# A hybrid of selective scan, attention and spectral filters: softplus in pairs, mixed matrices requested sooner, sums of y beside a filter's projection

## The chip, the cores and the metric

The kernel runs on one core of one Trainium2 chip. Its engines work in parallel, each through its own queue in order: TensorE (PE; its weight loads are listed as PEld), VectorE (DVE), ScalarE (ACT), GpSimd (POOL), and SyncE (SP), which here issues nearly all DMAs. The metric is the device time of one execution in microseconds (us). A change of under 0.2% can hardly be told from none.

## The reference, cut to what matters

Four images of 48 x 48 positions with 128 channels pass through a selective scan in four directions, self-attention, and a spectral filter layer. All numbers are float32.

```python
# layer 0, per image (L = 2304 positions, d = 256, K = 4 directions, N = 16 states, R = 8)
xz = einsum('bhwc,ec->bhwe', gn(x), in_proj_w);  xin, z = split(xz)
xc = silu(depthwise_conv3x3(xin))
xs = stack([rows, columns, rows reversed, columns reversed of xc])
x_dbl = einsum('bkdl,kcd->bkcl', xs, x_proj_w);  dts_r, Bs, Cs = split(x_dbl)
dt = softplus(einsum('bkrl,kdr->bkdl', dts_r, dt_proj_w) + dt_proj_b)
def step(h, inp):                         # for each position
    h = h * exp(dt_l * A) + (dt_l * u_l) * B_l
    y = einsum('bkdn,bkn->bkd', h, C_l)
...
x = x + out_proj(layernorm(sum over directions of y + Ds * xs) * silu(z))
# layer 1
t = t + softmax(ln(t) @ ln(t).T) @ ln(t)
# for each of four prefixes of the sequence, 16 filters phi, both signs:
U_plus, U_minus = causal convolutions of u = ln(t) with phi (and with alternating sign)
out = einsum('btkd,k,kde->bte', U_plus, s, Mpp) + einsum('btkd,k,kde->bte', U_minus, s, Mpm)
out = out + three shifted products of u with M_u
t = t + the prefixes' outs, weighted
```

## The kernel before

**Stages.** The program goes through the images (batches b = 0 to 3) one after the other. Each has a *scan stage* (`scans`) and then a stage of the scan's epilogue and attention, in which the prologue of the next image is worked in. Spectral filters of image b - 1 (`stu`) are done on PE beside the scans of image b, for b = 1 to 3; beside the scans of image 0 PE makes the mixed matrices `G` of all filters (`mixture`) and writes them to memory (`gd`). The filters of image 3 come alone at the end (`stu3`). Instructions stand in the order in which the Python code issues them; each engine works through its own part of that order.

**Scans.** An image has 24 *chunks* (4 directions x 6 stretches of 384 positions), and a chunk 8 *units* (2 halves of the channels x 4 groups of states), so 192 units in a stage. A unit is four scans on DVE (L517) over decays `exp(dt * A)` that ACT makes (L510), one instruction for each scan. The decays lie in the *ring*: 5 banks of PSUM for image 0, 4 for the others. The same banks take the spread rows of B (L493, a copy on ACT) and the small products of the chunk preparation. The scan's input dt*x*B is made by DVE (L501) or, for three of eight units, by POOL (same line). After the scans POOL multiplies by C (L527), and PE sums over the states (`sum_c`, L535, four matmuls with 32 columns each side by side); after four units DVE adds the sum to `ya` (L547; for image 0, ACT copies, L545). Scan tiles `s` are six deep, so a late sum keeps a tile from its next unit.

**Preparation.** `Chunk.prep` is a generator that runs 15 steps, each of three calls, over the units before its chunk; `LEAD` says that it starts 17 units ahead. It projects x to `xd` (L411, L418; for directions 2 and 3 `xd` is read back, L400), makes dt in two halves (L428, copy L431 into `re`), applies softplus (L440), multiplies by x (L458, DVE, into the other half of `re`), stores both as `dtdud` (L447), and loads them spread over the partitions as `rep` (L452, 8 DMAs per chunk). The rows B and C are requested by `fetch` (L479), four DMAs for each of 8 tiles `bc0` to `bc7` (one buffer each), as soon as a tile is free. Softplus and exp lie in different tables of ACT: an `ACT_TABLE_LOAD` stands ahead of each softplus and ahead of the next exponential.

**Filters beside the scans.** `stu` has 80 *items* (5 blocks of positions x 16 filters). Item n does: first Toeplitz product `conv(n, 0)` into bank `cx`; the projections of item n - 2 with `G` (`project`, L1224, two matmuls, one for each sign, the second after a call of `fetch` for the next Toeplitz tables `tt`, L1120); second product `conv(n, 2)`, accumulating in the same bank `cx`; third product `conv(n, 1)` in bank `cy`. ACT copies results away (`taken`): after the first product `cx` to `cy` (L1177), which the second product must wait for, after the second (L1184, L1185) and after the third (L1181) into `U`. These copies are issued 500 columns (`LATER`) of PE's later work after their product. `fetch_G` (L1131) requests `G` for item n - 1 after the first product of item n; `G` has two buffers.

**The weave.** In each unit step s, `scans` issues scan 0, work, the product with C of unit s - 1, scan 1, the addition to `ya`, work, scan 2, work, scan 3, the requests of `bc` (`refill`), the sum of unit s - 2 on PE, and work. "Work" is `more(share)`: it pulls pieces of `stu` until the columns done have reached that share of the stage. `prepare(s)` is called three times in the step.

**Before a scan stage.** The first chunks are prepared in the last slots of the attention before: `begin_scans` is called from slot `slots - BEGIN` (BEGIN = 23) on and yields once per slot. A slot is two matmul steps on PE and one exponential on ACT.

Of the kernel before, what the change touches and what calls it, by code (L numbers as in the profile page):

```python
# [15 lines left out]
P = 128  # L16
# [25 lines left out]
COPIES = 3  # L42
SHIFT = 55.0
LATER = 500


class Stage:
# [13 lines left out]
def hybrid_kernel(ctx: ExitStack, tc: tile.TileContext, a: dict, out: bass.AP):  # L61
# [9 lines left out]
    bank = {"turn": 0}  # L71

    ident = wp.tile([P, P], F32, name="ident")
    make_identity(nc, ident)
# [292 lines left out]
    class Chunk:  # L367


        def __init__(self, b, k, c):  # L370
            self.b, self.k, self.lo = b, k, c * CS
            self.name = f"{b}_{k}_{c}"
            self.bc, self.rep = {}, []
            self.rev = k >= 2
            self.first = c == (NCH - 1 if self.rev else 0)
            self.last = c == (0 if self.rev else NCH - 1)

            self.slot = CS if self.rev else 0
            self.at = slice(0, CS) if self.rev else slice(1, CS + 1)

        def prep(self, pool):
# [38 lines left out]
                mm_done(hold)  # L420
            yield from rest()

            re = pool.one.tile([P, NH, 2, CS], F32, tag="re", name=f"re{name}")
            for h in range(NH):
                hold = mm_hold()
                yield
                ps = mm_tile(f"dt{name}_{h}", hold)
                nc.tensor.matmul(ps[:, :CS], dtw[:, k, h * P:(h + 1) * P], xd, start=True, stop=True)  # L428
                yield CS
                yield  # L430
                nc.scalar.copy(re[:, h, 0], ps[:, :CS])  # L431
# [8 lines left out]
            nc.scalar.activation(re[:, :, 0], re[:, :, 0], AF.Softplus)  # L440
            yield
            yield
            yield 0
            d = dram.tile([NH, G4, DL, 2, CS], F32, tag="dtdu", name=f"dtdud{name}")

            def store(h):
                nc.sync.dma_start(d[h].rearrange("g j i t -> (g j) i t"), re[:, h])  # L447

            def load(h):
                rep = pool.rep.tile([P, G4, 2, CS], F32, tag="rep", name=f"rep{name}_{h}")  # L450
# [3 lines left out]

            for h in range(NH):
                x = in_order(xc[h], k, self.lo, CS)
                dt, dx = [re[:, h, i].rearrange("p (r w) -> p r w", w=x.shape[2]) for i in range(2)]
                nc.vector.tensor_tensor(dx, dt, x, ALU.mult)  # L458
            yield
            yield  # L460
            store(0)
# [88 lines left out]
    POOLED = ((0, 3), (1, 1), (1, 3))  # L550
    order = [(k, c) for k in range(K) for c in (range(NCH) if k < 2 else reversed(range(NCH)))]
    quads = [(h, q) for h in range(NH) for q in range(Q4)]
    STEPS = 15
    LEAD = 17
    FETCHED = range(2 * Q4)

    CHUNK_COLS = len(quads) * CS + 3 * CS

    def begin_scans(b, pool):

        chunks = [Chunk(b, k, c) for k, c in order]
        preps = [ch.prep(pool) for ch in chunks]
        for i in range(7):
            next(preps[0])
        for i in range(3 * STEPS - 7):
            if next(preps[0]) is not None:
                yield
        for i in FETCHED:
            chunks[0].fetch(i, pool)
        for i in range(3 * (LEAD - len(quads))):  # L570
            if next(preps[1]) is not None:
                yield
        for i in range(3 * (LEAD - 2 * len(quads))):
            next(preps[2])
        yield chunks, preps

    def scans(b, chunks, preps, front, sp, back, ring, finish, work, work_cols):
# [60 lines left out]
        for s in range(len(units) + 2):  # L638
            real = s < len(units)
            enter(s)  # L640
            prepare(s)
            if real:
                scan(s, 0)
            more((s + 0.25) / len(units))
            next(finish, None)
            if 1 <= s <= len(units):
                units[s - 1].times_c(s == len(units))
            if real:
                scan(s, 1)
# [417 lines left out]
    def stu(b, env, seeds):  # L1067
# [119 lines left out]
        def begin(n):  # L1187
            (lo, hi, place, extra), k = items[n]
            m = 2 if extra else 1

            now["x"] = pool.one.tile([P, 6, P], F32, tag="ux", name=f"ux{b}_{n}")
            nc.sync.dma_start(now["x"][:, 2:, :hi - lo], ud[:, :, 1 + lo:1 + hi])
            nc.sync.dma_start(now["x"][:, :2, :hi - lo], ud[:, 2:, lo:hi])
            now["mu"] = pool.one.tile([P, 2, 3, C], F32, tag="mue", name=f"mue{b}_{n}")
            nc.sync.dma_start(now["mu"][:, :m], mud[:, place:place + m])
            now["T", n] = pool.two.tile([P, 4, C], F32, tag="res", name=f"res{b}_{n}")
# [19 lines left out]
        def project(n):  # L1216
# [3 lines left out]
            for q in range(2):  # L1220
# [54 lines left out]
        fetch_G(n)  # L1275
        for i in (n - 1, n):
            yield from project(i)
            do_late()
# [231 lines left out]

    SB = bass.MemoryType.SB

    BEGIN = 23

    def run(tasks, lag, other):

# [33 lines left out]
    run(prologue(0, turn.one, mm_tile), 3, weights(once.one))  # L1550
    turn.close()
    once.close()
    front = Stage(tc, "f0", "left", one=(1, SB), xd=(3, SB), rep=(3, SB))
    first = begun(begin_scans(0, front))
    begin0.close()
    start_y(0)
    for b in range(B):
# [56 lines left out]
                parts.pop(0)()  # L1614
        if more:
            turn.close()
            front = Stage(tc, f"f{b + 1}", "left", one=(1, SB), xd=(3, SB), rep=(3, SB))
            start_y(b + 1)
            pieces = begin_scans(b + 1, front)
        first = None  # L1620
# [81 lines left out]
```

## Time and profile before

| what | value |
|---|---|
| three executions | 5554.54, 5556.91, 5560.95 us (median 5556.91) |
| profiled execution | 5558.94 us, span 5557.2 us |
| mean granted TensorE clock | 0.932 |
| before the first scan | 0 to 120 us |
| scan stages of images 0 to 3 | 948.5, 985.4, 988.3, 988.5 us |
| between them (epilogue, attention) | 247.1, 241.5, 242.4 us |
| after the last scan (attention, filters of image 3) | 795.5 us |
| DMA issues of SP in the page: bc, rep, dtdud | 3072 of 48 KB, 768 and 192 of 384 KB |
| table loads ahead of softplus and of exponentials | 95 and 89, 1283 ns each |

A profile row names line, engine, instruction, output<-inputs, shape and count. "Idle before" is the time for which the engine stood before such instructions, followed by what ended it. In a table of waits, "PE cx L1161 <- ACT cy L1177" reads: PE stood before matmuls of line 1161 until ACT had done its copy of line 1177. A PE product of float32 shows as two matmul records. The granted clock is near 1.0 in the scan stages of images 1 to 3 and 0.76 in that of image 0.

### The profile page before, as it was taken

What the parts mean: (1) busy time and instruction counts of PE and PEld (TensorE: products, weight loads), DVE (VectorE), ACT (ScalarE), POOL (GpSimd) and SP (SyncE); (2) the same over time, 40 slices, a digit from 0 to 9 for tenths busy, and PEclk for the clock granted to TensorE, in tenths of its full rate; (3) what the DMA queues carried; (4) which work ended last, traced back from release to release, by engine and by line L of the source; (5) the groups of instructions that cost most, each with busy time, mean ns of one, the idle gap of its engine ahead of it and who ended that gap; (6) DMA issues with size and microseconds to landing.
All of it is one profiled execution on the core that took longest, in us unless ns stands there. A gap on an engine that the chain in (4) does not pass through costs nothing. (4 is left out here: it accounts for less than half of the span.)

```text
span 5557.2 us, 73634 instructions
## 1 busy us (share of the span) xinstructions
PE 4768.0 (86%) x23372; PEld 3061.7 (55%) x23372; DVE 4338.2 (78%) x5307; ACT 3327.3 (60%) x6923; POOL 3660.4 (66%) x1882
## 2 busy tenths in 40 slices
PE   3566555698899999897899999997999999989999
PEld 1212111344666666644666666645666666659987
DVE  6999999855899999756999999657999999513211
ACT  2777767546777777456777776456777776432111
POOL 1899999714889998605888999406889999301100
PEclk6877777799999999998999999999999999999999
DMA  3545544305778787416787777326877787226543
GB/s 104 167 152 169 167 160 159 122 30 153 224 244 254 247 262 242 135 33 183 223 250 249 253 257 246 95 67 178 235 244 255 247 259 245 54 70 150 145 147 95
DMA packets 741419, 996.40 MB, mean 179 GB/s; under 512 B 142760, under 2 KB 565288, under 8 KB 740968
## 3 DMA queue, kind: packets, MB, share of 16 engines
q1 hardware_dynamic: 735208, 988.40, 57.8%
q10 hardware_dynamic: 5824, 3.30, 0.3%
q8 instruction: 187, 3.06, 0.2%
q14 instruction: 200, 1.64, 0.1%
HBM read 873.03 MB, written 118.31 MB: 178 GB/s over the span
## 5 line engine op out<-in xcount | busy, mean ns | idle before, releaser
L517 DVE TENSOR_TENSOR_SCAN s<-ring,s 128x385 f32<-128x385 f32 x3072 | 2697.4, 941 | 120.2 <-ACT ring L510 119.3
L527 POOL TENSOR_TENSOR s<-s,bc 128x1536 f32<-128x1536 f32 x764 | 2425.7, 3178 | 109.9 <-DVE s L517 55.2
L510 ACT ACTIVATE ring<-rep,A 128x384 f32<-128x384 f32 x3072 | 1759.1, 584 | 811.0 <-DVE s L501 472.1
L501 POOL TENSOR_TENSOR s<-rep,bc 128x1536 f32<-128x1536 f32 x288 | 993.9, 3451 | 161.6 <-DMA bc<-xdd 155.3
L501 DVE TENSOR_TENSOR s<-rep,ring 128x1536 f32<-128x1536 f32 x480 | 833.1, 1736 | 80.8 <-issue 35.9
L535 PE MATMUL y<-s,csum 128*32 128x384 f32 x6144 | 714.2, 539 | 180.5 <-POOL s L527 109.9
L1161 PE MATMUL cx<-tt,u 128*128 128x252 f32 (+7 forms) x2880 | 626.4, 360 | 105.8 <-ACT cy L1177 105.8
L1161 PEld LDWEIGHTS cx<-tt,u 128*128 128x128 f32 x2880 | 505.8, 194 | 319.7 <-ACT cy L1177 151.8
L1161 PE MATMUL cx<-tt,us 128*128 128x252 f32 (+7 forms) x2880 | 612.3, 355 | 53.6 <-ACT U L1185 33.5
L1161 PEld LDWEIGHTS cx<-tt,us 128*128 128x128 f32 x2880 | 493.7, 192 | 218.7 <-issue 96.9
L1161 PE MATMUL cy<-tt,u 128*128 128x252 f32 (+5 forms) x2880 | 603.8, 351 | 0.0
L1161 PEld LDWEIGHTS cy<-tt,u 128*128 128x128 f32 x2880 | 493.9, 191 | 149.8 <-issue 99.0
L1224 PE MATMUL pr<-U,G 128*128 128x288 f32 (+4 forms) x1344 | 438.5, 455 | 54.1 <-DMA G<-gd 54.0
L1481 POOL TENSOR_TENSOR t<-s,s 128x512 f32<-128x512 f32 x48 | 63.7, 1326 | 544.2 <-ACT s L1479 544.2
L535 PEld LDWEIGHTS y<-s,csum 128*32 128x32 f32 x6144 | 126.2, 112 | 511.9 <-issue 238.1
L823 ACT ACTIVATE e<-s,shift 128x512 f32<-128x512 f32 (+1 forms) x360 | 231.2, 644 | 284.1 <-PE s L821 283.7
L941 PE MATMUL G<-M,W 128*128 128x256 f32 (+3 forms) x512 | 233.2, 571 | 191.4 <-ACT W L931 82.4
L821 PE MATMUL s<-xnT 128*128 128x512 f32 (+1 forms) x720 | 342.2, 560 | 13.9 <-ACT xnT L781 13.9
L1224 PEld LDWEIGHTS pr<-U,G 128*128 128x128 f32 x1344 | 233.9, 192 | 199.6 <-issue 85.5
L813 PE MATMUL o<-e,xn 128*128 128x512 f32 (+1 forms) x720 | 337.3, 552 | 1.9 <-ACT e L823 1.9
L525 POOL COPY carry<-s 128x4 f32<-128x4 f32 x640 | 120.8, 189 | 304.3 <-DVE s L517 299.6
L941 PEld LDWEIGHTS G<-M,W 128*128 128x128 f32 x512 | 101.8, 231 | 320.2 <-issue 132.7
(236 smaller groups left out, 5183.1 us busy)
## 6 DMA issues: line engine op xcount, KB each, us to landing
rep<-dtdud SPq DMA_DIRECT2D x768, 384.0 KB
bc<-xdd SPq DMA_DIRECT2D x3072, 48.0 KB
tt<-fd SPq DMA_DIRECT2D x144, 577.0 KB
dtdud<-re SPq DMA_DIRECT2D x192, 384.0 KB
tt<-fd SPq DMA_DIRECT2D x144, 451.0 KB
tt<-fd SPq DMA_DIRECT2D x144, 325.0 KB
t<-fd SPq DMA_DIRECT2D x80, 384.0 KB
G<-gd SPq DMA_DIRECT2D x112, 256.0 KB
```

What stands on the lines that cost most here:

```text
L501: eng.tensor_tensor(s, self.ch.rep[self.h][:, :, 1], bt.unsqueeze(1).to_broadcast([P, G4, CS]), ALU.mult)
L510: nc.scalar.activation(ring.body(self.dA[g]), ch.rep[self.h][:, g, 0], AF.Exp, scale=A[:, ch.k, self.h * G4 + g, self.q:self.q + 1])
L517: nc.vector.tensor_tensor_scan(s, ring.decays(i, ch.rev), s, 0.0, ALU.mult, ALU.add)
L525: nc.gpsimd.tensor_copy(carry[:, self.h, self.q].unsqueeze(2), self.s[:, :, end:end + 1])
L527: eng.tensor_tensor(self.s, self.s, ch.bc[Q4 + self.q].unsqueeze(1).to_broadcast([P, G4, CS]), ALU.mult)
L535: nc.tensor.matmul(ch.y[g * DL:(g + 1) * DL, :CS], csum, self.s[:, g], start=(self.q == 0), stop=(self.q == Q4 - 1))
L813: nc.tensor.matmul(po[J][:, :w], xn[:, i], e[:, :w], start=(i == 0), stop=(i == NT - 1))
L821: nc.tensor.matmul(p[:, :w], xnT[:, i * P:(i + 1) * P], xnT[:, 512 * J:512 * J + w], start=True, stop=True)
L823: nc.scalar.activation(e[:, :w], p[:, :w], AF.Exp, bias=shift)
L941: nc.tensor.matmul(p[:, :n], W[:, q if t else 0, i], M[t][:, i].unsqueeze(1).to_broadcast([P, n, C]), start=(t == 0 and i == 0), stop=(t = ...
L1161: nc.tensor.matmul(p4[:, 1:3, v - (hi - at):] if g else p4[:, 0:4:3, v - (hi - at):], x, t[:, :, hi - 1 - at + J * P:end if end >= 0 else ...
L1224: nc.tensor.matmul(o if q else o.rearrange("p f r m -> p r f m"), G, U[n][:, 4 * q:4 * q + 4, v0:v1].rearrange("p (a b) m -> p a b m", a=2 ...
```

## The change

- Softplus: an even chunk of the order starts 5 units earlier and rests 5 units before its softplus; an odd chunk's softplus comes in the same call of `prepare`, right behind it, and rests 8 units afterwards. So two chunks' softplus stand next to each other on ACT. dt has two tiles (even, odd) and dt*x a third, so each store is two DMAs instead of one; `xd` has two buffers instead of three.
- The preparation before a stage goes further for the second chunk (softplus included) and the third, in a different interleaving, and begins 20 slots before the end instead of 23.
- `fetch_G(n)` is issued after the projections in item n, instead of `fetch_G(n - 1)` before them.
- The residual `res` of a block is loaded at its 15th filter instead of at its start, in one buffer instead of two.
- After the second projection matmul of an item, `stu` marks a *spot*. Two of the four work calls of a unit stop there; before the sum, `reach` runs work on by up to 1000 columns until a spot comes. So the sum is issued at the spot where one is near.

```diff
+REACH = 1000
...
-            re = pool.one.tile([P, NH, 2, CS], F32, tag="re", name=f"re{name}")
+            dt = pool.one.tile([P, NH, CS], F32, tag=f"dt{self.odd}", name=f"dt{name}")
...
-            nc.scalar.activation(re[:, :, 0], re[:, :, 0], AF.Softplus)
+            if not self.odd:
+                yield from rest(EARLY)
+            nc.scalar.activation(dt, dt, AF.Softplus)
+            if self.odd:
+                yield from rest(len(quads))
...
+            dx = pool.one.tile([P, NH, CS], F32, tag="dx", name=f"dx{name}")
...
             def store(h):
-                nc.sync.dma_start(d[h].rearrange("g j i t -> (g j) i t"), re[:, h])
+                for i, x in enumerate((dt, dx)):
+                    nc.sync.dma_start(d[h].rearrange("g j i t -> (g j) i t")[:, i], x[:, h])
...
-    STEPS = 15
-    LEAD = 17
+    EARLY = 5
+    STEPS = (15 + EARLY, 15 + len(quads))
+    LEAD = (17 + EARLY, 17 + len(quads))
...
+        DT = 23
+        for i in range(8, DT + 4):
+            go(0, min(i, DT))
+            go(1, i - 3)
+            if i % 3 == 2:
+                yield
+        go(0, DT + 3 * EARLY)
+        go(0, DT + 3 * EARLY + 1)
+        go(1, DT + 1)
+        ends = [3 * (LEAD[c % 2] - len(quads) * c) for c in range(4)]
+        ends[0] = 3 * STEPS[0]
+        yield
+        for i in range(DT + 3 * EARLY + 2, ends[0] + 1):
+            go(0, i)
+            go(2, min(i - DT - 3 * EARLY, ends[2]))
+            if i % 3 == 0:
+                yield
         for i in FETCHED:
             chunks[0].fetch(i, pool)
...
+        for c in range(1, 4):
+            go(c, ends[c])
...
-        def more(share):
-
-            while done[0] < share * total:
+        def more(share, hold=False):
+
+            while done[0] < share * total and not (hold and bank["spot"]):
...
+        def reach():
+
+            far = done[0] + REACH
+            while done[0] < min(far, total) and not bank["spot"]:
                 cols = next(work, None)
...
-            for c in range(ci + 1, ci + 4):
-                if c < len(chunks) and 0 <= s - len(quads) * c + LEAD < STEPS:
+            for c in range(ci + 1, ci + 5):
+                if c < len(chunks) and 0 <= s - len(quads) * c + LEAD[c % 2] < STEPS[c % 2]:
...
-            more((s + 0.5) / len(units))
+            more((s + 0.5) / len(units), True)
...
-            more((s + 0.75) / len(units))
+            more((s + 0.75) / len(units), True)
...
             if s >= 2:
+                if units[0].ch.b:
+                    reach()
                 units[s - 2].sum_c(back.psy)
...
+                bank["spot"] = q == 1
                 yield 4 * w
+                bank["spot"] = False
...
+            if k == KF - 2:
+                residual(n - k)
             yield from conv(n, 0)
-            if n > 0:
-                fetch_G(n - 1)
             if n > 1:
                 if k == 2:
                     yield from ar(n - 2)
                 yield from project(n - 2)
+            fetch_G(n)
             for c in (2, 1):
                 yield from conv(n, c)
...
-    BEGIN = 23
+    BEGIN = 20
...
-    front = Stage(tc, "f0", "left", one=(1, SB), xd=(3, SB), rep=(3, SB))
+    front = Stage(tc, "f0", "left", one=(1, SB), xd=(2, SB), rep=(3, SB))
```

More of the change, by code (lines that the diff above doesn't have):

```diff
@@ L70, in hybrid_kernel @@
     dram = ctx.enter_context(tc.tile_pool(name="dram", bufs=3, space=DRAM))
-    bank = {"turn": 0}
+    bank = {"turn": 0, "spot": False}
     ident = wp.tile([P, P], F32, name="ident")
@@ L367, in hybrid_kernel, with __init__ @@
     class Chunk:
-        def __init__(self, b, k, c):
+        def __init__(self, b, i, k, c):
             self.b, self.k, self.lo = b, k, c * CS
+            self.odd = i % 2
             self.name = f"{b}_{k}_{c}"
@@ L430, in prep @@
                 yield
-                nc.scalar.copy(re[:, h, 0], ps[:, :CS])
+                nc.scalar.copy(dt[:, h], ps[:, :CS])
                 mm_done(hold)
@@ L456, in prep @@
                 x = in_order(xc[h], k, self.lo, CS)
-                dt, dx = [re[:, h, i].rearrange("p (r w) -> p r w", w=x.shape[2]) for i in range(2)]
-                nc.vector.tensor_tensor(dx, dt, x, ALU.mult)
+                v, o = [y[:, h].rearrange("p (r w) -> p r w", w=x.shape[2]) for y in (dt, dx)]
+                nc.vector.tensor_tensor(o, v, x, ALU.mult)
             yield
@@ L559, in begin_scans, with go @@
     def begin_scans(b, pool):
-        chunks = [Chunk(b, k, c) for k, c in order]
+        chunks = [Chunk(b, i, k, c) for i, (k, c) in enumerate(order)]
         preps = [ch.prep(pool) for ch in chunks]
[L563 to L566, printed above, removed]
+        calls = [0] * len(preps)
+        def go(c, n):
+            for i in range(calls[c], n):
+                next(preps[c])
+            calls[c] = n
+        DT = 23
[14 more added lines that the diff above has]
+            if i % 3 == 0:
                 yield
@@ L569, in begin_scans @@
             chunks[0].fetch(i, pool)
[L570 to L574, printed above, removed]
+        for c in range(1, 4):
+            go(c, ends[c])
         yield chunks, preps
@@ L581, in scans @@
         done = [0]
-        def more(share):
-            while done[0] < share * total:
+        def more(share, hold=False):
+            while done[0] < share * total and not (hold and bank["spot"]):
+                cols = next(work, None)
+                if cols is None:
+                    break
+                done[0] += cols
+        def reach():
+            far = done[0] + REACH
+            while done[0] < min(far, total) and not bank["spot"]:
                 cols = next(work, None)
@@ L1195, in begin, with residual @@
             nc.sync.dma_start(now["mu"][:, :m], mud[:, place:place + m])
-            now["T", n] = pool.two.tile([P, 4, C], F32, tag="res", name=f"res{b}_{n}")
+        def residual(n):
+            (lo, hi, place, extra), k = items[n]
+            now["T", n] = pool.one.tile([P, 4, C], F32, tag="res", name=f"res{b}_{n}")
             nc.sync.dma_start(now["T", n][:hi - lo], td[4 * lo:4 * hi].rearrange("(p j) c -> p j c", j=4))
@@ L1274, in stu @@
         n = len(items) - 1
-        fetch_G(n)
         for i in (n - 1, n):
@@ L1616, in hybrid_kernel @@
             turn.close()
-            front = Stage(tc, f"f{b + 1}", "left", one=(1, SB), xd=(3, SB), rep=(3, SB))
+            front = Stage(tc, f"f{b + 1}", "left", one=(1, SB), xd=(2, SB), rep=(3, SB))
             start_y(b + 1)
```

## The prediction

> **What bounds the kernel now.** I read the busy table first, then the busy times of the four scan stages (windows from each batch's first scan to its last), then the waits of DVE and of PE in one of them, then the timeline around one softplus.
>
> ```profile
> PE 4768.0 (86%) x23372; PEld 3061.7 (55%) x23372; DVE 4338.2 (78%) x5307; ACT 3327.3 (60%) x6923; POOL 3660.4 (66%) x1882
> ```
> Over the whole span no engine is full. By stage it is different (the columns are stretch, length, then busy us of PE, PEld, DVE, ACT and POOL):
> ```profile
> 120.00:1068.50 948.50, 555.23 (x2246) 181.86 (x2246) 908.98 (x931) 670.89 (x1403) 869.15 (x422) 0.76 0.50 161
> 1315.60:2301.00 985.40, 917.30 (x5046) 625.69 (x5050) 925.92 (x994) 709.79 (x1526) 872.41 (x425) 0.98 0.76 235
> 2542.50:3530.80 988.30, 917.70 (x5046) 625.27 (x5049) 924.49 (x993) 710.17 (x1526) 872.47 (x425) 0.98 0.75 234
> 3773.20:4761.70 988.50, 918.06 (x5046) 625.91 (x5050) 925.99 (x993) 710.04 (x1526) 872.30 (x424) 0.98 0.75 234
> ```
> In the scans of batch 0, DVE is busy 909 of 948.5 us and PE has room. In those of batches 1 to 3 (mean 987.4 us) DVE has 925.5 us of work and PE 917.7: two nearly full engines, with 61.9 and 69.7 us idle. The waits of the second stage tell why (us in total, times, longest):
> ```profile
> DVE s L517 <- ACT ring L510: 34.6, 26, 4.4
> DVE s L501 <- issue: 12.1, 9, 6.7
> DVE ya L547 <- PE y L535: 7.5, 9, 2.5
> ...
> PE cx L1161 <- ACT cy L1177: 33.9, 22, 9.0
> PE pr L1224 <- DMA G<-gd: 17.1, 11, 4.3
> PE cx L1161 <- ACT U L1185: 10.9, 8, 3.0
> PE cx L1161 <- DMA tt<-fd: 7.1, 4, 2.8
> PE y L535 <- POOL s L527: 4.8, 2, 3.5
> ```
> PE hardly ever waits for something to sum (4.8 us); it waits for ACT's copy and for matrices. So PE is behind: from the end of POOL's product of a unit to the start of its sum the timeline shows a median of 4.5 us, against 1.8 us in batch 0. ACT in turn waits for PE's late results before it comes to the next exponentials, and DVE pays. One softplus, in the timeline (start, us, instruction, idle before):
> ```profile
> 1813.44 1.28 ACT L440 ACT_TABLE_LOAD   x1
> 1814.73 0.84 ACT L440 ACTIVATE re<-re 128x768 f32<-128x768 f32 x1
> 1815.60 1.28 ACT L510 ACT_TABLE_LOAD   x1
> 1816.89 1.09 ACT L510 ACTIVATE ring<-rep,A 128x384 f32<-128x384 f32 x2
> 1817.51 0.96 DVE L517 TENSOR_TENSOR_SCAN s<-ring,s 128x385 f32<-128x385 f32 x1 [0.91 <-ACT ring L510]
> ```
> From the first load to the end of the first exponential ACT gives no decay for 4.04 us. DVE lives on what the ring holds and then stands, here for 0.91 us. A scan stage has 22 such episodes; I added DVE's waits behind them: 5.9 us in batch 0, 30.6, 30.7 and 29.0 us after it, 1.37 us per episode.
>
> **Pairs of softplus.** The built order of ACT has 11 pairs where 22 singles stood, each pair at the place in the unit where every other single was. A pair is load, softplus, softplus, load: 4.04 + 0.84 = 4.88 us without a decay, on the same stock. DVE's wait per pair: 1.37 + 0.84 = 2.21 us, times 11 = 24.3 us against 30.1, if PE stays as late. Of the singles, those behind which ACT did not wait for PE cost about 0.55 us: with a punctual PE a pair costs 0.55 + 0.84, together 15.3. From above: if the ring is drained twice as deep, 2 x 1.37 + 0.84 = 3.58 each, 39.4. I take 22, since PE gets partly punctual (below). In batch 0 (0.27 us per episode) the same sum gives 11 x (0.27 + 0.84) = 12 against 5.9: 6 us lost. ACT is rid of 88 loads of 1.283 us in the scans, which nobody waits for beyond these episodes.
>
> Against the 1.283 us of the rows and the exponential that follows 0.01 us after the load, the Trainium skill (ScalarE: Activation LUTs, What ACT_TABLE_LOAD costs) adds 1.38 us of drain to each switch, 2.66 us in all. The trace shows no drain; by the page the two switches that a pair saves would be worth 2 x 1.38 us more, an estimate of 30 us per stage on top, which I leave out.
>
> **Mixed matrices sooner.** G's request moves from after the next filter's first product to before the filter's own second product: nearly two filters ahead instead of one. PE stood 17.1, 17.7 and 19.2 us for it, 15.8 of the first in the stage's first 185 us, where a filter lasts some 4 us (requests at 1319.43 and 1323.21). I take 15 us of PE per stage; between 0, if a queue in front is what delays it, and 18. The price: SP now stops at this request until PE has done the projection that frees the buffer (two matmuls, 1.85 us). Queued behind it on SP are bc (for ACT's spread and POOL), rep (for DVE and ACT) and the next tt (for PE). At most 80 x 1.85 = 148 us per stage; SP issues per chunk of 41 us about 32 bc x 0.62, 8 rep x 0.64, 10 tt x 0.53, 3.3 G x 0.55, some 33 us, so 24 x 8 = 190 us are free, and SP already waits for PE at tt (L1120), one product earlier. Nothing on the path; were only half of the free time of use, the 148 us and the 21 us of the split store below would leave 169 - 95 = 74 us per stage uncovered, bc would be late, and POOL with it.
>
> **Sums at the projection.** In PE's built order 60 of the 234 second products that follow a projection have a sum between; after the change 225. The sum is no dearer anywhere: from the end of what stands before it to the start of what follows the median is 0.71 us at every place in the filter work, the projection among them. Of the places without one, those directly behind the first product (90) waited 62.3 us for ACT's copy, the other 84 waited 10.7; the 54 with a sum waited 3.8, 0.07 each. For 165 places that get a sum, 73 x 165/174 less 165 x 0.07 leaves 58 us saved, 19 us of PE per stage. Bounds: 0, if the copy is simply later, and 35, all of that wait. The work held back (up to half a unit) or pulled forward (up to 1000 columns, 4 x 0.41 us by the 252-column products) shifts the sums; what could be late for that is L547 and the scan tiles, now 8.8 and 14.5 us per stage. Bounds for these: gone, or 48 x 1.64 = 79 us more.
>
> **Small parts.** The store of dt and dt*x becomes two DMAs: 48 more per stage at 0.44 us (L447, two in 0.88 us), 21 us of SP in the 190. Its lead before the first use is as before: 0. The residual moves to two filters before a block's end, some 10 us or more ahead of L1251: 0. Before a stage, the 32 bc requests (20.8 us of SP) start about 5 slots of 1.72 us before the attention ends instead of 10; the first spread comes at 1311, the first product with bc4 at 1319: just in time, 0, between -3 and +5 per stage. In batch 0 the second chunk's projection now lies ahead of the first store: +2.
>
> Against the split store speaks a rule of the Trainium skill (DMA: Bandwidth & Descriptors, Rules for kernel authors): coalesce many small transfers, since under 64 KB one pays mostly overhead. Each half here is 128 x 384 x 4 bytes, 192 KB, so even by the page the sum gets nothing for it; no row here shows such an overhead.
>
> **Sum.** PE: 917.7 + 69.7 - 15 - 19 = 953 us per stage. DVE: 925.5 + 22 for pairs + 4 other ring waits + 13 for what PE's lateness costs (L501, L547, L1251 are 26.2 now; half of it) = 964.5. The longer one decides: 987.4 - 964.5 = 23 us per stage. 3 x 23 = 69, less 6 and 2 in batch 0: 61. The profiled execution took 5558.9 us (span 5557.2), 2.0 above the median of 5556.9: 5558.9 - 61 - 2 = 5496 us. Its own range: 5465 (DVE at 925.5 + 22 + 4 + 2) to 5540 (a third of the 61).
>
> **Rivals.**
> - *Both clean*: PE gets punctual, pairs cost 15.3, the rest 8: DVE 949 us (and PE 947, if 6 of the 11 us for L1185's copy go too, which a punctual PE and an ACT with half the bursts allow), 38.4 per stage, 115 - 8 = 107, 5450 us. For it: batch 0 runs with 39 us of DVE idle. Against: PE and POOL (872 us, in order) would be at 95% and 92%.
> - *Off the path*: PE's saved waits come back at the sums as waits for POOL, as in batch 0 (93.9 us there); only the pairs' 6 us per stage reach DVE: 18 - 8 = 10 us, 5547. Against: DVE's waits for PE are there to be had.
> - *The pair drains the ring*: PE's copies queue behind a longer burst and the exponentials behind those copies, place L510 behind L440. Pairs cost 39.4, +9.3 per stage, in batch 0 2 x 0.27 + 0.84 = 1.38 each, +9.3; nothing else reaches the end: 4 x 9.3 + 2 = 39, 5596 us. It decides from 30.1 / 11 = 2.74 us per pair. For it: the worst singles already cost 3.9 to 4.4. Against: the typical one does not.
> - That the change does not do what it says is excluded by the built order.
>
> **Chances.** Likeliest 0.60, both clean 0.13, off the path 0.10, drained ring 0.17. Within 0.2% (11 us, what a measurement of this kernel can tell from none) falls the off-path case: same 0.09; slower 0.17; faster 0.74, the two first cases and a little. The range takes in the first two cases and most of the third: 5450 to 5556.
>
> **What would show it.** Right: 97 table loads instead of 191 (so the built order has it); L1224's wait for G near 3 us per stage; L1161's wait for L1177 near 16; stages near 964 us; product to sum under 3 us. Wrong: DVE's wait for L510 above 40 us per stage (drained ring), PE y waiting for POOL by tens of us at unchanged stages (off the path), or POOL and ACT waiting for bc (SP's stop).

## The result, and the profile after

| | before | changed |
|---|---|---|
| median of 12 executions each, us | 5555.1 | 5551.06 |
| lowest to highest | 5548.67 to 5560.95 | 5542.32 to 5557.82 |
| ratio to before, 95% interval | | 0.9993 [0.9985, 1.0001] |
| profiled execution (span) | 5558.94 (5557.2) | 5557.82 (5556.1) |
| up to the first scan | 120.0 | 122.1 |
| scan stage of image 0 | 948.4 | 949.8 |
| scan stages of images 1 to 3 | 985.3, 988.3, 988.4 | 980.2, 983.0, 977.2 |
| between stages | 247.2, 241.5, 242.4 | 252.4, 250.3, 247.4 |
| after the last scan | 795.5 | 793.8 |

No change that can be told from none. The sum by stage is: the three scan stages gained 21.6 us (69 were forecast), the stretches between them lost 19.0, and the start and image 0 lost 3.5. The busy table of the changed kernel, then its scan stages (columns as before: stretch, length, busy us of PE, PEld, DVE, ACT, POOL, granted clock, DMA share, GB/s):

```profile
PE 4748.2 (85%) x23372; PEld 3069.0 (55%) x23372; DVE 4324.8 (78%) x5307; ACT 3219.4 (58%) x6829; POOL 3651.1 (66%) x1882
```
```profile
122.10:1071.80 949.70, 556.56 (x2240) 184.57 (x2240) 903.10 (x930) 643.60 (x1379) 868.78 (x422) 0.74 0.48 157
1324.30:2304.50 980.20, 909.89 (x5040) 626.11 (x5044) 923.93 (x993) 684.70 (x1503) 872.53 (x425) 0.98 0.74 236
```
ACT is rid of 94 instructions, the table loads (191 to 97), and of 108 us. PE and DVE have the work that they had; PE still stands for 70 us of the second stage and DVE for 56. What they stand for has changed. The waits of that stage (us, times, longest):

```profile
DVE ya L555 <- PE y L543: 29.6, 16, 7.2
DVE s L525 <- ACT ring L518: 23.2, 21, 4.0
DVE s L509 <- DMA td<-T: 6.5, 1, 6.5
```
```profile
PE cx L1197 <- ACT cy L1213: 26.7, 12, 12.5
PE cx L1197 <- ACT U L1221: 18.7, 15, 2.9
PE cx L1197 <- DMA tt<-fd: 10.7, 6, 5.0
PE y L543 <- DVE ya L555: 7.7, 8, 1.8
PE y L543 <- POOL s L535: 6.4, 5, 3.5
...
PE pr L1263 <- DMA G<-gd: 2.7, 2, 2.5
```
PE's wait for G is gone, as forecast (17.1 to 2.7), and that for `cy` fell from 33.9 to 26.7. In their place stand the copies of U (10.9 to 18.7), `tt` (7.1 to 10.7) and the single bank of y (none to 7.7). On DVE the ring waits fell from 34.6 to 23.2, and the addition to `ya` now waits 29.6 us where it waited 7.5.

### The profile page after: what moved, and what is told of

It reads as the page before. It is cut to its first block, busy times and chain, and to the rows that moved or that the text cites. A ratio compares the mean times of both kernels' runs of the same rounds, so it can differ in the third digit from the quotient of the medians.

```text
span 5556.1 us, 74165 instructions
## 1 busy us (share of the span) xinstructions
PE 4748.2 (85%) x23372; PEld 3069.0 (55%) x23372; DVE 4324.8 (78%) x5307; ACT 3219.4 (58%) x6829; POOL 3651.1 (66%) x1882
## 3 DMA queue, kind: packets, MB, share of 16 engines
q14 instruction: 205, 1.68, 0.1%
## 5 line engine op out<-in xcount | busy, mean ns | idle before, releaser
L535 POOL TENSOR_TENSOR s<-s,bc 128x1536 f32<-128x1536 f32 x764 | 2427.3, 3180 | 94.3 <-DVE s L525 33.3
L509 POOL TENSOR_TENSOR s<-rep,bc 128x1536 f32<-128x1536 f32 x288 | 994.5, 3453 | 195.7 <-DMA bc<-xdd 163.5
L509 DVE TENSOR_TENSOR s<-rep,ring 128x1536 f32<-128x1536 f32 x480 | 830.9, 1731 | 64.1 <-DMA td<-T 21.1
L1197 PE MATMUL cx<-tt,u 128*128 128x252 f32 (+7 forms) x2880 | 595.8, 355 | 82.5 <-ACT cy L1213 82.2
L1197 PE MATMUL cy<-tt,u 128*128 128x252 f32 (+5 forms) x2880 | 583.7, 347 | 8.6 <-DMA tt<-fd 8.5
L1197 PEld LDWEIGHTS cy<-tt,u 128*128 128x128 f32 x2880 | 495.1, 191 | 99.0 <-issue 44.7
L1522 POOL TENSOR_TENSOR t<-s,s 128x512 f32<-128x512 f32 x48 | 63.4, 1321 | 520.6 <-ACT s L1520 520.6
```

The source lines that it names most:

```text
L509: eng.tensor_tensor(s, self.ch.rep[self.h][:, :, 1], bt.unsqueeze(1).to_broadcast([P, G4, CS]), ALU.mult)
L535: eng.tensor_tensor(self.s, self.s, ch.bc[Q4 + self.q].unsqueeze(1).to_broadcast([P, G4, CS]), ALU.mult)
L1197: nc.tensor.matmul(p4[:, 1:3, v - (hi - at):] if g else p4[:, 0:4:3, v - (hi - at):], x, t[:, :, hi - 1 - at + J * P:end if end >= 0 else ...
```

## The experiments

The lengths below are those of each run's profiled execution: mean of the scan stages of images 1 to 3, sum of the three stretches between stages ("gaps"), and per stage DVE's waits at the addition and for the ring. Ratios are to the kernel before on the same chip.

| run | ratio [95%] | stages | gaps | addition | ring |
|---|---|---|---|---|---|
| before | 1 | 987.3 | 731.1 | 8.8 | 35.0 |
| changed | 0.9993 [0.9985, 1.0001] | 980.1 | 750.1 | 28.7 | 21.4 |
| e1 pairs alone | 0.9972 [0.9961, 0.9982] | 981.4 | 741.6 | 16.3 | 31.6 |
| e2 G alone | 0.9991 [0.9982, 0.9999] | 986.9 | 729.2 | 11.5 | 40.4 |
| e3 moved sums alone | 0.9995 [0.9986, 1.0003] | 985.8 | 733.0 | 19.5 | 24.7 |
| e4 pairs and G | 0.9976 [0.9966, 0.9986] | 983.2 | 746.1 | 14.8 | 32.0 |
| e5 changed, earlier start | 0.9977 [0.9967, 0.9987] | 981.5 | 733.4 | 29.2 | 22.4 |
| e6 changed, later addition | 1.0024 [1.0015, 1.0033] | 990.5 | 745.9 | 4.4 | 53.5 |
| e7 less PE | 0.9981 [0.9973, 0.9990] | 978.8 | 745.7 | 25.8 | 23.4 |
| e8 less DVE | 0.9893 [0.9880, 0.9906] | 978.3 | 740.1 | 52.4 | 27.1 |
| e9 less PE and DVE | 0.9858 [0.9836, 0.9879] | 970.0 | 741.8 | 44.7 | 31.0 |
| e10 e4 with less PE | 0.9961 [0.9948, 0.9975] | 976.1 | 741.5 | 13.4 | 27.6 |
| e11 e1, earlier start | 0.9948 [0.9936, 0.9961] | 978.0 | 731.0 | 13.9 | 31.6 |
| e12 e5, less pulled ahead | 0.9971 [0.9960, 0.9983] | 983.5 | 730.4 | 14.6 | 33.3 |
| e13 less PE, DVE and POOL | 0.9830 [0.9815, 0.9844] | 966.9 | 736.2 | 40.5 | 34.3 |
| e14 less POOL | 0.9915 [0.9899, 0.9932] | 975.7 | 737.8 | 34.5 | 22.2 |
| e15 changed, one bc request | 0.9862 [0.9846, 0.9879] | 964.8 | 720.1 | 16.8 | 19.3 |
| e16 before, one bc request | 0.9918 [0.9903, 0.9933] | 975.3 | 730.0 | 3.2 | 31.1 |
| e17 e9, one bc request | 0.9555 [0.9541, 0.9569] | 921.8 | 731.5 | 9.5 | 20.3 |
| e18 e11, one bc request | 0.9832 [0.9817, 0.9847] | 959.7 | 725.4 | 1.8 | 28.2 |

### The parts one by one (e1 to e4)

e1 takes these lines out of the changed kernel; e4 only the first two pairs; e2 and e3 put the one or the other group into the kernel before.

```diff
-            more((s + 0.5) / len(units), True)
+            more((s + 0.5) / len(units))
...
-                if units[0].ch.b:
-                    reach()
...
+            if n > 0:
+                fetch_G(n - 1)
...
-            fetch_G(n)
```


> Pairs of softplus alone, with their earlier preparation (G requested as before, sums where they were). Theory 1 (the changed kernel gave back what the pairs won in two places: DVE's addition to ya waits for sums that were moved, 28.7 us per stage instead of 8.8, and each later stage starts 5 to 9 us late because the store of T stands behind the 32 bc requests on SP): DVE's wait for L518 falls to about 17 us per stage as in the changed kernel, its wait at the addition stays near 9, the late start stays; 3 x 18 won, 19 + 5 lost: about 30 us faster than before (ratio 0.9946). Rival (PE is what bounds the stages, the pairs only move DVE's wait to another place): ratio 1.000 to 1.004, stages as long as before and the wait back at the addition or at the scan tiles.

> The earlier request of G alone. Theory 1: PE's wait for G falls from 17 to 19 us to under 3 per stage; some 10 us per stage reach the end, 30 us in all (ratio 0.9946), no new wait. Rival (off the path): the wait turns up as PE waiting for ACT or for tt, ratio 0.999 to 1.001.

> The sums at the projection alone. Theory 1: PE's wait for ACT's copy falls by some 10 us per stage, but DVE's wait at the addition to ya grows from 9 to about 29 per stage; slower than before by 10 to 40 us (ratio 1.002 to 1.007). Rival (the sums are placed well, the addition's wait has another cause, such as the pairs): the addition's wait stays near 9, 20 us faster or more (ratio below 0.9965).

> The changed kernel without the moved sums: pairs and the earlier G. Theory 1: the addition's wait falls back to about 9 us per stage, stages of 980 us fall to about 965; the late start stays: 45 us faster than before (ratio 0.992). Rival (moved sums are neutral): as the changed kernel, ratio 0.9985 to 1.000, the wait at the addition near 29.

Pairs alone are the one part that pays, 15 us by the medians (5561.15 to 5546.13), though their stages start later like the changed kernel's (gaps +10.5). G alone takes 15 us of waits per stage off PE and gives 4 (by the median) in all: PE's wait for `cy` rises from 34 to 37 us to 41. The moved sums alone take 9 us off `cy` and bring 11 at the addition. Whatever is taken from one wait stands at the next. Against what was expected: e2 fell to its rival; e1, e3 and e4 came out between their first theory and their rival, with the wait at the addition at 16.3, 19.5 and 14.8 us and not near 9 or 29.

### The start of a stage, and the addition (e5, e6, e11, e12)

In SP's timeline of the changed kernel and in DVE's, ahead of the second stage:

```profile
1295.67 22.76 SPq L487 DMA_DIRECT2D bc<-xdd  x32
1318.53 0.56 SPq L1098 DMA_DIRECT2D ud<-uT  x1
1319.51 0.37 SPq L1065 DMA_DIRECT2D td<-T  x1
```
```profile
1322.58 1.75 DVE L509 TENSOR_TENSOR s<-rep,ring 128x1536 f32<-128x1536 f32 x1 [6.52 <-DMA td<-T]
```
The scan tile of DVE's second product uses the memory of T, which the attention's last store must have read. That store stands in SP's queue behind 32 bc requests, which now start at 1295.67 and not at 1287.95: it goes out at 1319.51 (before: 1311.04), and DVE stands for 6.52 us. e5 and e11 are `BEGIN = 26` in the changed kernel and in e1. e6 and e12 (the latter on e5) are

```diff
-            if pending:
-                pending.pop().add_y()
...
             if real:
                 scan(s, 3)
+            if pending:
+                pending.pop().add_y()
```
```diff
-                if units[0].ch.b:
+                if units[0].ch.b and units[s - 2].q < Q4 - 1:
                     reach()
```


> The changed kernel, with the preparation of a batch's scans begun six attention slots earlier (BEGIN 26 for 20); nothing else. Theory: the gaps between the scan stages grew from 247.2, 241.5 and 242.4 us to 252.4, 250.3 and 247.4 because SP meets the 32 bc requests (22.8 us) ahead of the store of T, and both the first scan and the scan tile behind that store come late; with the earlier start the first scan comes 6 to 9 us earlier in batches 1 to 3, DVE's wait at L509 for the store of T (6.5 us in the second stage) shrinks below 1 us, and the ratio to before is 0.9965 (5.7 us per batch less than the changed kernel). Rival: the first scan is set by the end of the attention's own work on PE and ACT, and the gaps were lengthened by something else; gaps within 2 us of the changed kernel's, ratio 0.9985 to 1.000.

> The changed kernel, with DVE's addition of a chunk's y (L555) issued one scan later within its step; nothing else. Theory: the sums that a projection holds back or pulls forward make PE's sum late for an addition that stands in DVE's queue ahead of ready scans; one scan later (about 2 us of DVE more) most of these waits end: L555 falls from 28.7 us per stage to under 15, and a stage gets 8 to 15 us shorter (ratio 0.994 to 0.997). Rival: DVE and PE go at a common pace, and the wait only turns up elsewhere (at the scan's exponentials, or at PE's wait for the y bank): L555 falls all the same, stages stay within 3 us of 980.2, 983.0 and 977.2, ratio 0.998 to 1.000.

> Pairs alone (G and sums as before), with the preparation begun six slots earlier (BEGIN 26). Theory: the pairs' gain in the stages (4 to 7 us each) and the earlier start (5 us per gap, as the changed kernel showed) add up: gaps 245, 241 and 242 us, ratio to before 0.995 to 0.996. Rival: with SP's old order of G and tt in front, the earlier requests collide with the attention's tail: gaps as with pairs alone (249.6, 244.8, 247.2), ratio 0.997.

> The changed kernel with BEGIN 26 and no work pulled ahead of the last sum of a chunk, the one that DVE's addition waits for. Theory: the wait at the addition falls from 28 us per stage to under 18, that for the ring stays at 23; if DVE is one of two walls and PE the other, the stages get only 0 to 5 us shorter, ratio 0.995 to 0.998. Rival: the addition's wait is what bounds, and the stages follow it by 10 us or more, ratio under 0.993.

The earlier start gives back the gaps: 750.1 to 733.4 and 741.6 to 731.0 us (731.1 before). The first theory of e5 and of e11 holds for the start (DVE's wait for the store of T falls to 0.4 us or less); e5's ratio stays short of its 0.9965, since its stages are 1.4 us longer. For the addition e6's rival holds, and e6 is worse than that: the addition's wait goes, but it frees the one bank of y late (PE's waits for it rise from 7 to 25 us), and the ring's wait rises to 53.5. e12 met neither of its forecasts: the addition's wait falls by half, the ring's rises by 11, and the stages are 2 us longer.

### Taking work away (e7 to e10, e13, e14)

```diff
-                for v0, v1, x in parts(w, extra):
+                for v0, v1, x in parts(w, extra)[:0 if q else 2]:
```
```diff
-                nc.vector.tensor_tensor(o, v, x, ALU.mult)
```
```diff
             eng = nc.vector if last else nc.gpsimd
+            if self.q == 1:
+                return
             eng.tensor_tensor(self.s, self.s, ch.bc[Q4 + self.q]...
```
The first (in `project`) makes e7 and, on e4, e10; the second e8; both e9; the third e14, and all three e13.

> The changed kernel without the second of the two projection products of each filter (q = 1 of L1263), so the output lacks that half of the filters' terms: PE has about 234 x 0.2 = 47 us less to do per stage, all else stays. If PE's work sets the stage's length: stages 40 us or more shorter, 935 to 943 us. If DVE's work and its waits for ACT set it: within 10 us, 970 to 983. If the two engines hold each other up by turns: half of it, 955 to 965, with DVE's waits for PE at the addition and for ACT's ring both smaller.

> The changed kernel without DVE's product of dt and x (L466; dt is stored in its place, so the output is computed with dt for dt*x): DVE has about 24 x 1.9 = 46 us less to do per stage, all else stays. If DVE's work sets the stage's length: stages 35 to 46 us shorter, 935 to 945 us, and batch 0's, where PE has room, shorter by as much. If PE's work sets it: batches 1 to 3 within 10 us of 980, DVE's new idle time at the addition and the scans' exponentials; batch 0 shorter all the same. If by turns: 955 to 965 in batches 1 to 3.

> The changed kernel without the second projection product of each filter and without DVE's product of dt and x (both things that were left out one at a time in the two runs before; 47 us of PE and 36 us of DVE less per stage as those runs showed). Theory, two walls of one height: PE with its waits for ACT's copies needs some 978 us by itself, DVE with its pairs and its waits for sums needs some 978 us by itself, and taking from one alone shows the other. Then both together shorten the stages of batches 1 to 3 by 30 to 40 us, to 938 to 950. Rival, a third thing sets the pace (ACT's order, POOL with 872 us, or the shares by which the filter work is dealt out): stages stay above 965 us. If the engines only hold each other up by turns: between, 950 to 965.

> Pairs and earlier G, sums at the old place, without the second projection product of each filter (output lacks those terms): PE has 47 us less to do per stage, with no work held back or pulled forward around a sum. Theory: DVE's waits at the addition that stayed at 25 to 27 us per stage when the changed kernel lost the same PE work come from the work pulled ahead of the sums and not from PE's load; here they fall to under 10 us, the wait for the ring to 25, and the stages to 960 to 968 us (against 977 to 980 with the moved sums). Rival: those waits are there whenever DVE is nearly full, whatever the place of the sum: addition 15 us or more, stages 973 us or more.

> As the run without the second projection product and without dt*x, and also without POOL's product with C for every fourth unit (q = 1, whose sum takes the states as they are): POOL has 48 x 3.18 = 153 us less per stage, besides the 47 us of PE and 36 us of DVE. If POOL was the third wall: the stages of batches 1 to 3 fall from 970 to 940 us or less, and DVE's wait at the addition from 45 us to under 20. If the order of the work, with ACT in it, holds them: 960 us or more.

> The changed kernel without POOL's product with C for every fourth unit (q = 1), nothing else: POOL 153 us less per stage. If several engines stand within a few per cent of each other (PE, DVE and POOL with their waits), one alone gives little: stages 970 to 980 us. If POOL alone holds them: 950 us or less, with PE and DVE both less idle.

47 us less of PE: stages 1.3 us shorter. 36 us less of DVE: 1.8. Both: 10.1. 153 us less of POOL: 4.4. All three engines: 13.2. e7 and e8 each came out as forecast for the case that the other engine sets the length, which cannot be so for both; e14 as forecast for several engines within a few per cent. e9 fell to its rival, e13 to its rival: with the three full engines relieved, something else held the stages. (The largest part of what e8, e9, e13 and e14 won over the changed kernel lies in image 0, where PE has room: 905 to 928 us there instead of 950.) e10 was a miss: without the moved sums the addition still waits 13.4 us, not under 10, and the stages are not shorter than 974.

What else? I followed the releases back from the last scan of each stage to its first, by the rule of the page's chain (to what released an instruction, or else to the one before it on its engine), and added up where that chain lies; releases that the profile dates after the start that they should explain were passed over. SP's requests and DMAs in flight together, us in the three stages:

```
before   424  232  301      after  328  329  459
e9       629  519  634      e13    652  513  717
e15       35   30   42      e17     46   82   69
```
The sizes hang on that rule: the figures above pass over releases dated more than some 0.06 us late, and a looser rule, which passes over a release only if its instruction starts later than the one that it explains, gives 152 to 281 before, 129 to 242 after, 242 to 397 in e9 and e13, and 19 to 87 in e15 and e17. What stands under either rule is the distance between four bc requests and one, and not the order of before and after. The chain of the page ends in the filters after the last scan and shows none of this.

In the second stage of the changed kernel SP issues 1321 requests that take 742 us, 736 of them for bc at 0.58 us each, with 78 us in the short pauses between. SP is not full: 151 us are left. In part of these SP stands for its own transfers: the requests of SP signal on eight semaphores in turn, and 5682 of the 5749 of the execution first wait for the landing that used theirs last, eight requests earlier. For such landings SP waits 85 us in this stage (before 97, e9 98, e15 11, e17 13). And its queue is in order, and this is what it does to PE (SP's and PE's timelines of the changed kernel):

```profile
1743.53 1.17 SPq L1167 DMA_DIRECT2D G<-gd  x1
1745.48 0.36 SPq L1156 DMA_DIRECT2D tt<-fd  x1
1746.32 5.20 SPq L487 DMA_DIRECT2D bc<-xdd  x8
1751.56 0.57 SPq L1236 DMA_DIRECT2D res<-td  x1
1752.23 0.38 SPq L1156 DMA_DIRECT2D tt<-fd  x1
```
```profile
1757.65 0.76 PE L1197 MATMUL cx<-tt,us 128*128 128x252 f32 x1 [5.00 <-DMA tt<-fd]
```
Two `tt` requests that are due one after the other are 6.75 us apart, since eight bc requests and the residual lie between. PE stands for 5.00 us until the second has landed.

### One bc request for four (e15 to e18)

```diff
-            for c in range(C4):
-                row = 64 * (self.k // 2) + 32 + 4 * i + c
-                nc.sync.dma_start(t[c::C4], src[row].partition_broadcast(DL))
+            row = 64 * (self.k // 2) + 32 + 4 * i
+            v = src[row:row + C4]
+            nc.sync.dma_start(t, bass.AP(tensor=v.tensor, offset=v.offset, ap=[[0, DL]] + [list(z) for z in v.ap]))
```
The same bytes go to the same places, as 192 KB at once and not as four times 48.

> The changed kernel with one request for each bc tile in place of four (L487; same bytes, same values): SP has 552 requests x 0.58 = 320 us less per stage of its 755. If SP's queue is the wall behind PE's and DVE's: PE's waits for tt (11 us) and part of those for ACT fall, the bc requests ahead of a batch's first scan shrink from 22.8 to some 6 us and the gaps between stages with them, by 5 to 10 us; stages 960 to 970 us, ratio 0.985 to 0.993. If the transfers or the order hold the stages: 977 to 983 as now, and only the gaps shrink, ratio 0.996.

> The kernel before with the same one request per bc tile. If SP's queue hid what the change's other parts are worth, the changed kernel with one request is faster than this one by 10 us or more per stage, as the prediction had it (20 us); if the order holds both, the two stand as the kernels with four requests do (7 us per stage). Its own stages: 975 to 980 us if SP is the wall, 985 to 988 if not.

> The changed kernel without the second projection product and without dt*x, with one request per bc tile. If SP's queue was the third wall: the stages of batches 1 to 3 fall from 970 to 945 us or less, and DVE's wait at the addition from 45 to under 25. If the transfers or the order of the work hold them: 960 us or more.

> Pairs alone with the preparation six slots earlier (the fastest so far, 0.9948) and one request per bc tile. If the requests were in its way: stages 965 to 972 us and gaps 240 or less, ratio 0.982 to 0.990. If not: 0.994 to 0.996.

e17 decides: the stages that stood at 970.0 with less work on PE and DVE go to 921.8, and the addition's wait from 44.7 to 9.5. The same 47 us of PE and 36 us of DVE were worth 10.1 us per stage with four requests (980.1 to 970.0) and are worth 43.0 with one (964.8 to 921.8). So the third wall was the number of requests on SP's queue and not the bytes, which moved faster (239 GB/s in e9's second stage, 252 in e17's). Nor did the matrices travel faster: where the profiles date the landing, a `tt` request of the second stage lands after a median of 4.70 us in the changed kernel and 4.78 in e9, both with four bc requests, and after 4.54 in e16 and 4.95 in e18, with one (those of e15 and e17 date none). The run does not part the two things that a request costs, its 0.58 us on SP and its turn among the eight in flight: 552 requests fewer took both away, 317 us of bc requests (423.6 to 106.2) and 74 us of waits for landings. How SP stands to PE shows it best. SP's waits in the second stage of the changed kernel, where landings of its own earlier requests come first (the bc requests waited 78 times for a `rep` load, 39.5 us in all), and its waits for PE at the `tt` requests there and in e15:

```profile
SPq L487 <- DMA rep<-dtdud: 39.5, 78, 1.8
SPq L487 <- DMA tt<-fd: 18.1, 27, 1.6
...
SPq L1156 <- PE cy L1197: 13.7, 12, 4.6
SPq L1156 <- PE cx L1197: 12.5, 19, 1.9
```
```profile
SPq L1156 <- PE cx L1197: 228.2, 99, 7.3
SPq L1156 <- PE cy L1197: 86.5, 50, 8.6
```
With four requests SP waits for a Toeplitz product at 31 of the 188 `tt` requests and mostly comes to them after PE has freed the buffer, so the matrix is asked for late. With one it stands there ahead of PE at 149, and no wait of PE for `tt` is left in the stage:

```profile
PE cx L1197 <- ACT U L1221: 20.6, 16, 3.1
PE cx L1197 <- ACT cy L1213: 20.4, 12, 6.1
PE y L543 <- DVE ya L555: 9.0, 7, 3.1
```
And the change is worth something now: 5512.97 us (e16) to 5477.99 (e15), 35 us instead of 4, with stages 10.5 us shorter each (7.2 with four requests) and gaps 9.9 shorter in all where they were 19.0 longer. That is half of the forecast's 23 per stage, and of the 31 us that the change gains by the shorter queue the gaps bring 29 and the stages 10, and the rest of the execution takes 8 back. e16 fell to its first case, though barely (10.5 for "10 us or more"), and e15 and e17 to theirs. e18 is the fastest, 5463.65 us, 96 below the 5559.39 of the kernel before, measured beside it, and its stages are shorter than the 965 to 972 expected. It has neither the earlier G nor the moved sums, and its stages are 5 us shorter than e15's: its addition waits 1.8 us instead of 16.8, and PE's wait for G is 3 to 6 us though its request is where it was.

## Why the prediction was wrong, point by point

It forecast 5496 us, a clear gain; the median is 5551, within its range (5450 to 5556) and nearest to its rival "off the path" (5547, chance 0.10). Three slips in its working change nothing: a third of the 61 us gives 5537 and not 5540, 917.7 of 949 us is 97% and not 95%, and SP's requests of a chunk take 30.6 us and not 33 (7.8 `tt`, not 10).

- **The step that failed is the sum**, "The longer one decides: 987.4 - 964.5 = 23 us per stage". The stages came to 980.1 on average. Of DVE's terms, work and ring were about right ("22 for pairs + 4 other ring waits", measured 21.4). Wrong was "13 for what PE's lateness costs", half of the 26.2 at L501, L547 and L1251: the same three places cost 32.1 (28.7 at the addition, 2.2 and 1.2). That alone makes 979 of the 980. PE's 953 came to 980 too: G and `cy` gave 14.4 and 7.2 us in the second stage, and other waits took their place.
- **Under the sum lies a cover** that failed: SP's "24 x 8 = 190 us are free", "Nothing on the path". The number was about right (151 us are left), and the reading was wrong: an in-order queue that is 84% full of requests and their pauses, with at most eight requests in flight, delays each request by what stands in front of it. So a stage had a third limit close behind PE and DVE: e7, e8, e9 and e13 show it by what they did not give, e15 to e17 by what fewer requests gave. The prediction took the waits of PE and DVE as theirs to save, and did not follow a chain inside a stage. For the change itself this is about half of what is missing: with the shorter queue it gives 35 us and not 4, of 61 forecast, most of it between the stages. Inside them it gives 10.5 us and not 7.2, of 23; the rest stays at the addition, where e15 waits 16.8 us and e16 3.2. One thing about SP was as bounded: its stop at G until PE is through costs 21.7 us in the second stage, of 148 allowed.
- **Moved sums**: "19 us of PE per stage" against a lateness of which "half" was to go. The bound "48 x 1.64 = 79 us more" held the truth, and I took the other side. The addition waits 20 us more per stage than before. The example with the longest wait, 7.2 us, has the products of L1251 (`ar`) and the projection ahead of the sum that DVE stood for. That the moved sums do this is shown by e3 (the sums alone, 8.8 to 19.5), by e12, where nothing is pulled ahead of a chunk's last sum (29.2 to 14.6), and by e18 without them (1.8). Product to sum stayed at a median of 4.4 to 4.9 us (forecast: under 3), in e15 too.
- **G sooner**: the wait fell as forecast (15 of 17 us), but not the time (e2). The bound named with it, "0, if a queue in front is what delays it", fits e18, where the wait falls to 3 to 6 us with the old request and a shorter queue (13 to 16 in e11, the same with four requests); but e16, with the shorter queue and the old start, keeps 11 to 13.
- **Pairs**: a mechanism that was right. An episode takes 4.77 us (forecast 4.88; two softplus in a row take 1.58 and not 1.68), and DVE waits 12.3 us per stage behind the eleven (forecast 22, 15.3 with a punctual PE; PE did not get punctual), and 20.4 in e1, with the pairs alone. In image 0 it is 8.9 (forecast 12). e1 gave 5.9 us per stage, as the off-path rival had it, and e4 4.1. The first pair of a stage (us: start, length):

```profile
1359.88 1.28 ACT L444 ACT_TABLE_LOAD   x1
1361.17 1.58 ACT L444 ACTIVATE dt<-dt 128x768 f32<-128x768 f32 x2
...
1362.85 1.28 ACT L518 ACT_TABLE_LOAD   x1
1364.15 1.09 ACT L518 ACTIVATE ring<-rep,A 128x384 f32<-128x384 f32 x2
```
- **Before a stage**: "just in time, 0, between -3 and +5" was 6.3 us per stage (1.7 to 5.0 in the other runs with that start and four bc requests). I followed the bc requests to their own users, and not what stands behind them on SP: the store of T.
- **The rivals.** "Off the path" had the size right and the place wrong: PE's saved waits did not come back as waits for POOL (4.8 to 6.4 us in the second stage) but at U, `tt`, the bank of y and DVE's addition. "The pair drains the ring" is refuted by 1.1 us per pair, and 1.9 in e1, where it began at 2.74. That G or the sums would pay once the queue is free is not shown: e18 without them beats e15. What of e15's gain over e16 belongs to the pairs alone was not tried at the same start.

The rule weighed in the prediction (the Trainium skill, DMA: Bandwidth & Descriptors, Rules for kernel authors: coalesce small transfers, below 64 KB one pays mostly overhead) was dismissed for the split store of 192 KB. It bore on another row: the bc requests are of 48 KB, 3072 in all, and joining four of them gave the kernel before 46 us (5559.39 to 5512.97). What the runs show of the overhead is the request's time on SP's queue and its turn there.

## What to carry to other kernels

A queue of requests is an engine: count its requests, their pauses and its waits for earlier landings in each stage, and look whether it waits for its consumers or they for it, before calling anything hidden behind its free time. Where two engines are nearly full and both wait, take work away from each and from both; if the stage does not move, follow the releases back within the stage. A store that frees memory for the next stage belongs on the path as much as a load.

## What the hardware showed that was not expected

- A bc request of four times the bytes to four times the partitions costs SP no more: 0.58 us on average for 48 KB to 32 partitions (736 in the changed kernel's second stage), 0.58 for 192 KB to 128 (184 in e15's).
- DVE's product dt*x (L466, two operands in SBUF) never ran beside a long POOL instruction: 138 of 192 ran clear of them at 0.67 us, none wholly beside one, and the 54 that met one took 1.75 us on average, up to 3.4. Its other product (L509), which reads the ring, took 1.73 us with a long POOL instruction beside it for nine tenths of its time or more (323) and 1.75 alone (5). Without a quarter of POOL's products (e14) all 192 ran clear, at 0.68 us, and DVE was busy 24 us less in image 0. The Trainium skill (GPSIMD Engine Reference, 8. Key points) says that GpSimd shares its SBUF interfaces with VectorE and contends with instructions of two SBUF inputs; the rows agree.
